# When in an attention step the spread 3x3 operations are handed to the vector engine

## The chip, the cores and the metric

The kernel runs on one core of a Trainium2 chip. The metric is the device time of one execution in microseconds; the time before is the median of three runs, 3276.86 us (3268.33 to 3284.32). The core has a matrix engine (PE in the profile, with its weight loads as PEld), a vector engine (DVE), a scalar engine (ACT), a GpSimd engine (POOL) and a sync engine (SP) that only issues DMAs here.

## The reference, cut to what matters

Eight images of 512 channels and 32x32 pixels, all in float32. Layer 0 adds to the image a block that works on its group norm; layer 1 adds a masked 1x1 convolution of the group norm of that sum. The change touches only the inner part of layer 0, which runs twice per image (two blocks):

```
for i in range(N):                       # N = 2 blocks
    yi = ys[-1]
    z = cbs(yi, m_cv1_w[i], m_cv1_bn[i], 1)              # 3x3 convolution, norm, SiLU
    z = bot_attention(z, m_qkv_w[i], m_rw[i], m_rh[i])   # 4 heads, 1024 tokens
    z = silu(bn_eval(conv2d(z, m_cv2_w[i], 0), m_cv2_bn[i]))
    ys.append(yi + z)
```

The attention takes softmax over 1024 keys of `q (k + r) / 8` and multiplies with `v`. The 3x3 convolution has 256 channels in and out.

## The kernel before, in words

**Slots and units.** The work is cut into 16 slots, one for each image and block, in the order (image p, block 0), (image p+1, block 0), (image p, block 1), (image p+1, block 1) for each of the four pairs of images. Each slot has four attention units: a pair of heads `hp` and one half of the queries. While the units of one slot run, the convolutions of the next slot and of other images fill the matrix engine in between.

**A unit.** `top` transposes the running maxima (`mx`) on the matrix engine into a PSUM tile `mt`, and the vector engine reduces it to `nm` (L513, L514). `spread` brings these maxima back over the partitions as `mb` (L521). Then there are four steps, t = 0, 2, 4, 6, of two key tiles each. A step emits, in this order: `soften` of two tiles of this unit (the vector engine adds `mb`, L525; the scalar engine takes the exponential, L526; GpSimd adds to the sum `acc`, L531), `values` of the step before (matrix engine into `po`, L537), and `logits` of two tiles of the next unit: four matmuls `lg` (L494), each into its own PSUM bank, four scalar copies `st<-lg` (L500), and four maxima on the vector engine, `mx = max(mx, lg)` (L505; none for the first tile). A bank is free again once its copy and its maximum have read it. There are five such banks (`ps_f`), shared with all convolutions.

**The fill.** After each step `advance` runs a generator of other work until a share of the slot is done. That work is conv3 (the 3x3 convolution), the projections to q, k and v, `conv_m2`, and background items of other images (L175 for all 1x1 convolutions, L297 for the 3x3 products).

**The 3x3 convolution.** It is done in a Winograd form along the rows. `transform` computes eight vector operations, `a`, `b`, plane 1 and plane 2 (L264 to L267), then `a2`, `b2`, plane 3 and plane 4 (L269 to L272). `conv3` multiplies six planes in turn with `product`. After product 4, four more vector operations combine results (L340 to L343); L351 and L355 add products 0 and 5.

**Clock and Spread.** The order in which the program is written out is steered by a planner's clock. `clock.tick(us)` moves it on and calls everything that has fallen due. The operations of `transform` and of the combination are a `Spread`: each is put on the clock with its own due time (`delay + gap * n`), so that they don't come in one burst, and `upto` calls those that are needed before they are due. Group norm parts (`mean`, `var`, `norm_x` with L165) are put on the clock too. Most scheduling of instructions within an engine is then done by the tile framework from the order of emission, but the vector operations of `soften`, `logits` and `Spread` are chained in the order in which they were emitted:

```
def in_turn(instruction):
    if turn:
        tc.add_manual_dep(instruction.ins, turn.pop().ins.name, IN_ORDER, reason="order of VectorE")
    turn.append(instruction)
```

Other names that matter below: L441 and L139 add a residual and take its statistics in `conv2`; L471 adds a residual in `last` and reads its PSUM bank; L556 and L558 divide by the sum.

## Time and profile before

| | before |
|---|---|
| median of three runs | 3276.86 us |
| the profiled execution | 3278.47 us |
| its span on the core | 3276.7 us |
| PE busy | 3159.1 us (96%), 11716 matmuls |
| DVE busy | 2045.9 us (62%), 2717 instructions |
| ACT busy | 1756.6 us (54%), 2369 instructions |
| POOL busy | 1219.1 us (37%), 971 instructions |
| granted clock of the matrix engine | 0.99 |

Idle time of PE is what remains of the span, 117.6 us. A line of the waits view names an engine and its line, what ended the wait, and then the total in us, the number of times and the longest. A line of the timeline has start, length in us, engine, source line, operation, tiles, a count of merged instructions, and in brackets the idle time before the first and what ended it. The length of matmuls is modelled.

The slots are periodic: after the first pair of images, the same pattern comes again every 734 us or so (for instance the same transposes `mt` start after the same wait at 1205.1, 1940.7 and 2673.0 us).

### The profile page before, as it was taken

How to read it: one execution, taken by the hardware profiler on the slowest of the kernel's cores; microseconds unless marked ns; L12 is line 12 of the kernel's file. 1: busy time of each engine (PE TensorE's matmuls, PEld its weight loads, DVE VectorE, ACT ScalarE, POOL GpSimd, SP SyncE). 2: the span in 40 equal slices, each digit the busy share in tenths (PEclk: the TensorE clock that was granted, in tenths of full speed). 3: DMA queues.
4: the chain of work that ended last, by engine and by line, in shares of the span. 5: the costliest groups of instructions: out<-in, count | busy, mean ns of one | idle time of the engine just before them, and what ended most of it. 6: DMA issues, size and time to landing. Idle time of an engine off the chain costs nothing.

```text
span 3276.7 us, 33257 instructions
## 1 busy us (share of the span) xinstructions
PE 3159.1 (96%) x11716; PEld 1538.0 (47%) x11716; DVE 2045.9 (62%) x2717; ACT 1756.6 (54%) x2369; POOL 1219.1 (37%) x971
## 2 busy tenths in 40 slices
PE   7999999998999999999999999999999999999998
PEld 3645345353545445354545445354445444453343
DVE  5436566666666575767666675767656676666642
ACT  3245765854545655644545555644655554646631
POOL 2104433335334343344334343444334433444420
PEclk9999999999999999999999999999999999999999
DMA  8752352330323241423323341423333341423366
GB/s 292 275 171 71 119 170 94 116 106 20 121 98 106 75 148 55 161 84 106 122 98 105 104 144 54 161 84 108 124 105 108 101 141 49 160 71 116 111 217 205
DMA packets 142007, 399.30 MB, mean 122 GB/s; under 512 B 13072, under 2 KB 14352, under 8 KB 141840
## 3 DMA queue, kind: packets, MB, share of 16 engines
q1 hardware_dynamic: 141120, 396.94, 36.1%
q8 instruction: 93, 1.52, 0.2%
q14 instruction: 74, 0.61, 0.1%
q10 hardware_dynamic: 720, 0.23, 0.0%
HBM read 317.42 MB, written 79.69 MB: 121 GB/s over the span
## 4 chain that ended last, share of the span: by engine, by line
PE 69%; DVE 11%; issue 5%; ACT 4%; DMA 4%; POOL 1%; POOLq 0%; SPq 0%; ACTq 0%; DVEq 0%
PE cv L175 14%; PE m L297 12%; PE po L537 11%; PE lg L494 10%; PE qk L175 6%; PE l L175 5%; PE v L389 3%; DVE st L525 3%; PE mt L513 2%; PE m L175 2%; DVE rb L556 2%; DVE mx L505 2%; PE den L549 2%; PE mb L521 2%; DMA x<-in_x 1%
## 5 line engine op out<-in xcount | busy, mean ns | idle before, releaser
L531 POOL TENSOR_TENSOR sum<-sum,st 128x512 f32<-128x512 f32 x768 | 973.9, 1299 | 771.5 <-ACT st L526 771.5
L526 ACT ACTIVATE st<-st 128x1024 f32<-128x1024 f32 x512 | 534.3, 1056 | 471.4 <-DVE st L525 464.8
L505 DVE TENSOR_TENSOR mx<-mx,lg 128x512 f32<-128x512 f32 x768 | 479.3, 681 | 434.1 <-ACT st L500 433.6
L500 ACT COPY st<-lg 128x512 f32<-128x512 f32 x1024 | 528.1, 594 | 246.1 <-PE lg L494 189.9
L525 DVE TENSOR_TENSOR st<-st,mb 128x1024 f32<-128x1024 f32 x512 | 604.2, 1213 | 79.8 <-PE mb L521 79.8
L297 PE MATMUL m<-plane,w_m 128*128 128x256 f32 x2304 | 534.0, 386 | 18.0 <-DVE z L351 8.3
L494 PE MATMUL lg<-q,k 64*128 64x512 f32 x2048 | 534.6, 618 | 10.4 <-ACT rb L551 3.3
L537 PE MATMUL po<-st,v 128*64 128x512 f32 x2048 | 509.5, 609 | 17.2 <-ACT st L526 11.4
L297 PEld LDWEIGHTS m<-plane,w_m 128*128 128x128 f32 x2304 | 431.4, 191 | 142.7 <-issue 40.8
L531 POOL TENSOR_TENSOR sum<-st,st 128x512 f32<-128x512 f32 x128 | 162.2, 1288 | 834.1 <-ACT st L526 712.0
L175 PE MATMUL cv<-y,w_cv 128*128 128x512 f32 x1024 | 466.5, 600 | 4.9 <-DVE mx L505 2.1
L494 PEld LDWEIGHTS lg<-q,k 64*128 64x128 f32 x2048 | 188.9, 186 | 346.2 <-issue 236.5
L175 PEld LDWEIGHTS cv<-y,w_cv 128*128 128x128 f32 x1024 | 185.5, 190 | 252.0 <-issue 231.6
L537 PEld LDWEIGHTS po<-st,v 128*64 128x64 f32 x2048 | 125.2, 136 | 327.6 <-issue 231.6
L556 DVE RECIPROCAL rb<-rb 128x256 f32<-128x256 f32 x128 | 216.1, 1725 | 66.0 <-ACT rb L551 66.0
L175 PE MATMUL cv<-x,w_cv 128*128 128x512 f32 x512 | 242.2, 622 | 12.3 <-DVE mx L505 4.1
L175 PE MATMUL l<-x,w_l 128*128 128x512 f32 x512 | 235.2, 604 | 9.6 <-DVE mx L505 6.2
L175 PE MATMUL qk<-z,w_qkv 128*128 128x512 f32 x512 | 234.2, 600 | 1.6 <-DVE mx L505 1.6
L514 DVE TENSOR_REDUCE nm<-mt 128x4 f32<-128x512 f32 x128 | 83.0, 685 | 221.5 <-PE mt L513 221.2
L130 ACT ACT_TABLE_LOAD x122 | 156.5, 1283 | 14.7 <-PE m L175 6.4
L175 PEld LDWEIGHTS cv<-x,w_cv 128*128 128x128 f32 x512 | 97.0, 197 | 138.7 <-issue 112.1
L175 PEld LDWEIGHTS l<-x,w_l 128*128 128x128 f32 x512 | 93.3, 191 | 133.6 <-issue 106.5
(144 smaller groups left out, 2342.1 us busy)
## 6 DMA issues: line engine op xcount, KB each, us to landing
w_m<-w_m SPq DMA_DIRECT2D x96, 768.0 KB, 4.4
w_cv<-in_cv SPq DMA_DIRECT2D x90, 512.0 KB, 3.5
y<-y SPq DMA_DIRECT2D x64, 512.0 KB, 4.7
x<-in_x SPq DMA_DIRECT2D x56, 512.0 KB, 5.2
y<-y SPq DMA_DIRECT2D x64, 256.0 KB, 3.6
k<-r SPq DMA_DIRECT2D x32, 512.0 KB, 3.8
res<-y SPq DMA_DIRECT2D x32, 512.0 KB, 4.2
xr<-in_x SPq DMA_DIRECT2D x32, 512.0 KB, 4.3
```

The lines of the kernel that those rows point to most:

```text
L130: nc.scalar.activation(dst, src, AF.Silu, bias=bn_b[:, col : col + 1], scale=bn_s[:, col : col + 1])
L175: nc.tensor.matmul(ps, w, moving, start=(n == 0), stop=(n == len(terms) - 1))
L297: nc.tensor.matmul(ps[:, ts(co, 256)].rearrange("p (t x) -> p t x", x=F), w[:, co, c, dx], u[:, 9 * c : 9 * c + 8, dx : dx + F], start=(j ...
L389: nc.tensor.matmul(ps[:, ts(j, P)], z[:, c, ts(4 * j4 + j, P)], w[:, c, 512 + P * hp : 512 + P * hp + P], start=(c == 0), stop=(c == IT - 1),)
L494: nc.tensor.matmul(lg[h], self.k[r, ts(t, P)], self.q[r, self.hp, ts(self.half, HALF)], start=True, stop=True)
L500: nc.scalar.copy(st[:, h], lg[h])
L505: in_turn(nc.vector.tensor_tensor(self.mx[:, h], so_far[:, h], lg[h], ALU.max))
L525: in_turn(nc.vector.tensor_tensor(st, st, flat(self.mb), ALU.add))
L526: nc.scalar.activation(st, st, AF.Exp)
L531: nc.gpsimd.tensor_tensor(self.acc[:, h], so_far[:, h], self.st[t][:, h], ALU.add)
L537: nc.tensor.matmul(self.po[HD * h : HD * h + HD], self.v[:, t, ts(h, HD)], self.st[t][:, h], start=(t == 0), stop=(t == KT - 1),)
L556: nc.vector.reciprocal(self.rb[:, r], self.rb[:, r])
```

## The change

In the loop over the steps, the clock was moved on by 2.0 us after `values` and by another 2.0 us after `logits`. Now it is moved on once, after both. An operation that falls due during the first 2.0 us used to be emitted between `values` and `logits`; it is now emitted after `logits`, so behind its four maxima in the chain of the vector engine. The planner's time at the end of the step is the same.

```
                 if t:
                     u.values(t - 2)
                     u.values(t - 1)
-                    clock.tick(2.0)
                 if nxt:
                     nxt.logits(t)
                     nxt.logits(t + 1)
-                    clock.tick(2.0)
+                clock.tick((2.0 if t else 0.0) + (2.0 if nxt else 0.0))
                 advance((base + 4 + t) / steps)
```

More of the change, by code (lines that the diff above doesn't have):

```diff
@@ L1024, in conv_preact_kernel @@
                     u.values(t - 1)
-                    clock.tick(2.0)
                 if nxt:
@@ L1028, in conv_preact_kernel @@
                     nxt.logits(t + 1)
-                    clock.tick(2.0)
+                clock.tick((2.0 if t else 0.0) + (2.0 if nxt else 0.0))
                 advance((base + 4 + t) / steps)
```

## The prediction

> **What bounds the kernel now.** I read the page first, then the waits of PE, then the timeline at every place where the change moves an instruction.

> ```profile
> span 3276.7 us, 33257 instructions
> PE 3159.1 (96%) x11716; PEld 1538.0 (47%) x11716; DVE 2045.9 (62%) x2717; ACT 1756.6 (54%) x2369; POOL 1219.1 (37%) x971
> ...
> L505 DVE TENSOR_TENSOR mx<-mx,lg 128x512 f32<-128x512 f32 x768 | 479.3, 681 | 434.1 <-ACT st L500 433.6
> ```

> PE is the bound: it is idle for 117.6 us of the span, and only that can be won. The maxima mostly wait for the copy of the same bank (433.6 of 434.1 us), so an operation in front of them often costs nothing. The waits of PE:

> ```profile
> PE mt L513 <- DVE mx L505: 10.7, 3, 3.6
> PE m L297 <- DVE z L351: 8.3, 8, 2.1
> PE l L175 <- DVE mx L505: 6.2, 5, 1.5
> PE cv L175 <- DVE mx L505: 6.2, 6, 2.5
> PE m L297 <- DVE mx L505: 6.2, 5, 1.8
> ```

> With three smaller rows (1.6, 1.0 and 0.7) PE waits 32.6 us for maxima, because they free a bank or feed the transposes. That is the pool for the gain; a later operation of the vector engine can add to it.

> [...] L269 takes 712 ns at least and 1802 ns at most, the latter beside the sums L531 (about 1.1 us of waiting, then its own 0.7).

> **The change, part by part.** It adds and removes no instruction. In the built instruction lists, 30 of 2717 vector instructions move behind four maxima (4 x 0.6 us), in 18 places; POOL's and SP's queues, with all DMAs, are unchanged, ACT has swaps in seven places, PE a few. The other Spread operations fall due in the fill. I group the places by pattern and work each from the timeline, letting each operation start when the queue ahead, its copies (L500) and the lock allow. PE's gate (the matmul whose wait stands in brackets) after minus before is the price.

> *Three places at 1200, 1935, 2668 (L269 and L270 moved).*

> ```profile
> 2666.99 0.68 DVE L441 TENSOR_TENSOR xr<-xr,cv2s 128x512 f32<-128x512 f32 x1
> 2667.60 1.80 DVE L269 TENSOR_TENSOR a<-ybuf 128x544 f32<-128x544 f32 x1
> 2669.32 0.68 DVE L139 BATCH_NORM_STATS2 st_b<-xr 128x6 f32<-128x512 f32 x1
> 2669.92 1.18 DVE L270 TENSOR_TENSOR b<-ybuf 128x544 f32<-128x544 f32 x1
> 2671.03 2.47 DVE L505 TENSOR_TENSOR mx<-mx,lg 128x512 f32<-128x512 f32 x4
> ...
> 2672.95 1.97 PE L513 MATMUL mt<-ident,mx 128*128 128x128 f32 x8 [3.56 <-DVE mx L505]
> ```

> PE waits 3.56 us for the third maximum. Without L269 and L270 (1.80 + 1.18, less overlap) L139 ends at 2668.3, the copies (from 2668.07) are ready at 2668.6, and the maxima start at 2668.7 instead of 2671.0: 2.3 us. Behind them L269, L270, L271, L272 end at about 2675.0, so the reductions L514 end 0.2 us later than before, but the matmul that needs them (`mb`) stands behind 12 products (4.6 us) and doesn't wait. Gain 3 x 2.3 = 6.9.

> *Three places at 1375, 2110, 2842 (L265, L266).*

> ```profile
> 2848.10 2.48 DVE L505 TENSOR_TENSOR mx<-mx,lg 128x512 f32<-128x512 f32 x4 [3.42 <-ACT st L500]
> ...
> 2854.87 2.34 DVE L525 TENSOR_TENSOR st<-st,mb 128x1024 f32<-128x1024 f32 x2
> 2857.13 2.47 DVE L505 TENSOR_TENSOR mx<-mx,lg 128x512 f32<-128x512 f32 x4
> ...
> 2857.87 1.35 PE L297 MATMUL m<-plane,w_m 128*128 128x256 f32 x5 [1.35 <-DVE mx L505]
> ```

> Here the moved pair ran in a hole: the maxima waited 3.42 us for copies anyway, so they gain nothing. Behind them the pair takes 2 x 0.7, and from 2850.5 to 2859.6 the queue is full. The next maxima come 1.4 us later, and the PE gate at 2857.87 with them. Loss 3 x 1.4 = 4.1.

> *Two places at 1508, 2242 (L266, L267).*

> ```profile
> 2244.54 5.92 POOL L531 TENSOR_TENSOR sum<-sum,st 128x512 f32<-128x512 f32 x4 [3.18 <-ACT st L526]
> ...
> 2246.08 1.54 DVE L269 TENSOR_TENSOR a<-ybuf 128x544 f32<-128x544 f32 x1
> 2247.55 1.79 DVE L270 TENSOR_TENSOR b<-ybuf 128x544 f32<-128x544 f32 x1
> ...
> 2254.59 1.98 PE L175 MATMUL l<-x,w_l 128*128 128x512 f32 x4 [1.46 <-DVE mx L505]
> ```

> Before, L266 and L267 ran free (0.64 us apart) ahead of the sums. Afterwards the maxima are 1.3 us earlier, but PE waits for no bank there except one l matmul that the list moves ahead (its 0.85 us is lost again at the next gate). L266, L267, L269 and L270 then alternate with the four sums, at 1.6 to 1.75 each; L272 ends 1.95 us later, and so do L525, the next maxima and the gate. Loss 2 x 1.95 = 3.9.

> *Three places at 944, 1681, 2415 (L267).* The queue's tail keeps its end within 0.1 us (the lock only changes its victim). The first copy of the next step is moved ahead of an exponential, so the first maximum doesn't wait 0.46 us for it, and the gate (0.70) comes 0.45 earlier. Gain 1.4.

> *Four places at 505, 1428, 2162, 2896 (L341, and L351 one L525 earlier).* L341 to L343 end 0.8 us later behind the lock, L351 stands one L525 (1.13) earlier: PE's gate on L351 (0.65) comes 0.3 earlier. The second exponential and its copies are 1.4 later, but 24 products (5.4 us) cover that. Gain 1.3.

> *At 454 (L265, L266):* the exponentials come 0.9 to 1.2 later, but a copy is moved in front of the table load, and the gate (1.78) opens 0.7 earlier. *At 657 (L269, L270):* the maxima waited 1.97 us for copies; the reductions end 1.3 later, just covered by 12 products: 0. *At 772 to 806 (L264, L267, L271):* L525 comes 0.8 and then 2.1 later, partly behind POOL's release of buffers, and PE's gates on the exponential (4.44 and 3.04) about 1.1 in sum. *At 246* three L165 go behind copies on ACT; PE doesn't wait: 0.

> Sum: 6.9 + 1.4 + 1.3 + 0.7 - 4.1 - 3.9 - 1.1 = 1.2 us saved. The profiled execution would be 3278.5 - 1.2 = 3277.3; it is 1.6 above the median of the runs shown, so **3275.7** for the median. That is no change: 0.5% (16.4 us) is about what a measurement of this kernel can tell from none, and the three runs alone span 15.9.

> Bounds of what I can't see: the first group gives 0 (if the `nm` reductions become the gate) to 10.7 (the whole wait); the losses 0 (hidden after all) to about twice (a second gate); the stretch at 772, where ACT, POOL and DVE wait in turn, 2 us gained to 5 lost.

> **The rivals.** *Tails hidden.* If the second, third and last terms of loss cost nothing, 1.2 + 9.1 = 10.3 is saved: 3266.6. For it speaks that DVE is busy for only 62%; against it that at these places its queue has no hole until the gate. Over 0.5% needs 16.4 of 32.6 us, more than the gated time that moves; only scatter takes it there.

> *Tails gate (slower).* The postponed operation lands beside the four sums of its step, is locked out for 1.1 us, and the next L525, exponential, copy, maximum and bank come 1.95 later as at 2242. This passes 0.5% when 9 of the 18 places pay 1.95 and the gains are eaten; with 10, 3276.9 + 19.5 = 3296.4. For it speak PE's waits behind full queues; against it that I find locked tails with a gate in two places, unlocked ones in three.

> *Nothing moves that counts.* Order changes, gates don't: 3276.9. Only 1% of the vector instructions move. It can't be told from my forecast and shares its chance.

> **How the numbers follow.** Forecast with the null case 0.56; tails hidden 0.22, of which 0.06 lies beyond 0.5%; tails gate 0.22, of which 0.16 does. So faster 0.06, same 0.78, slower 0.16. The range runs from 3264 (tails hidden and a little scatter) to 3291 (tails gate at 7 places): 8 in 10.

> **What would show it.** Right: the waits of PE for `mx` at `mt` (3 x 3.57) fall to about 1.2 each; the waits at 1390, 2124, 2858 grow from 1.35 to about 2.8, those at 1521, 2255 from 1.47 to about 3.4 (less any lead that PE has by then, or more by it). Busy times of PE, ACT and POOL stay. Wrong: if the places at 505 or 944 lose time, if PE's idle time in sum changes by over 10 us, or if a wait appears away from the 18 places.

## The result and the profile after

The changed kernel takes **3287.2 us** (median of 8 runs, 3283.8 to 3294.3) against 3279.6 us before (8 runs, 3268.3 to 3284.3). The ratio is 1.0029 [1.0016, 1.0042]: slower by 9.5 us [5, 14], where the forecast was 1.2 us faster. (Microseconds beside a ratio are the ratio times the median before; the two medians alone differ by 7.6.) The change is smaller than the 0.5% that the prediction took for the least that can be told from none, but with eight runs on each side it is a loss and not a null.

From the page of the kernel after, its span, the busy times and the group of the maxima:

```profile
span 3283.5 us, 33262 instructions
...
PE 3167.8 (96%) x11716; PEld 1535.8 (47%) x11716; DVE 2044.9 (62%) x2717; ACT 1757.7 (54%) x2369; POOL 1216.6 (37%) x971
...
L505 DVE TENSOR_TENSOR mx<-mx,lg 128x512 f32<-128x512 f32 x768 | 480.2, 682 | 449.5 <-ACT st L500 449.2
```

The idle time of PE, span less busy time, fell from 117.6 to 115.7 us, in sum nearly as forecast. But its **busy** time rose by 8.7 us with the same 11716 matmuls. So the loss isn't in waiting: the same matmuls take longer. The waits of PE after (what ended the wait, total us, times, longest):

```profile
PE m L297 <- DVE mx L505: 9.7, 5, 2.7
...
PE lg L494 <- DVE x2r L471: 6.2, 2, 3.1
...
PE mt L513 <- DVE mx L505: 3.7, 3, 1.2
PE mb L521 <- DVE nm L514: 3.5, 3, 1.2
```

The wait of `mt` has gone from 10.7 to 3.7 us, that of L297 for maxima has grown from 6.2 to 9.7. Two rows are new: `lg` waits for L471 (6.2 us), and `mb` for the reductions (3.5 us).

**Where busy time grows.** A stop is idle time of PE in front of a matmul. The timeline at the third place of 1375/2110/2842 shows the stop, first before:

```profile
2857.87 4.15 PE L297 MATMUL m<-plane,w_m 128*128 128x256 f32 x18 [1.35 <-DVE mx L505]
```

Then in the kernel after, with the windows view for the clock behind the stop (columns: stretch, us, busy us and count of PE, PEld, DVE, ACT, POOL; then granted clock, DMA share, GB/s):

```profile
2857.22 1.98 PE L175 MATMUL l<-x,w_l 128*128 128x512 f32 x4
2861.95 5.84 PE L297 MATMUL m<-plane,w_m 128*128 128x256 f32 x18 [2.75 <-DVE mx L505]
```

```profile
2862.90:2866.30 3.40, 3.40 (x9) 2.70 (x8) 1.50 (x4) 0.00 (x0) 3.40 (x3) 0.50 0.04 14
2866.40:2870.40 4.00, 4.00 (x23) 2.44 (x22) 0.65 (x5) 0.00 (x0) 0.00 (x0) 1.00 0.00 0
```

Before, the same 18 products took 4.15 us after a stop of 1.35 us. After a stop of 2.75 us they take 5.84: the granted clock is 0.50 for 3.4 us, which I call a window of half clock, and half of that is lost (5.84 - 4.15 = 1.7). So 1.4 us of stop cost 3.1 us of time.

To price every place, I took the same matmul ahead of it and behind it in both traces. The stretch between them divides into idle time, the loss to the half clock (half of PE's busy time in windows with a granted clock of 0.50), and the rest (busy time less that loss). These are differences of the two profiled executions in us; negative is time saved:

| places | forecast | measured | idle | half clock | rest |
|---|---|---|---|---|---|
| 1200, 1935, 2668 | -6.9 | -9.1 | -3.5 | -7.3 | +1.7 |
| 1375, 2110, 2842 | +4.1 | +9.1 | +4.4 | +4.8 | -0.1 |
| 1508, 2242 | +3.9 | +7.4 | +1.5 | +6.8 | -1.0 |
| 772 to 806 | +1.1 | +3.1 | -1.6 | +0.5 | +4.1 |
| 944, 1681, 2415 | -1.4 | -1.6 | -1.6 | 0 | 0 |
| 505, 1428, 2162, 2896 | -1.3 | -1.6 | -1.6 | 0 | 0 |
| 454 | -0.7 | -0.4 | -0.7 | 0 | +0.3 |
| 657 | 0 | +0.2 | 0 | 0 | +0.2 |
| sum of these places | -1.2 | +7.0 | -3.1 | +4.8 | +5.2 |
| first to last matmul compared | | +7.0 | -1.7 | +2.0 | +6.7 |

What lies away from these places comes to nothing in sum, but out of parts: +1.4 of idle time, -2.8 of half clock and +1.5 of rest. Windows of half clock come and go there too: in all there are 14 before and 16 after, of 67.8 and 67.7 us. So the half clock is not longer in total. The change moves it: the losses at 1375, 1508 and 772 with their like (12.1 us) are largely offset by the gain at 1200 and its like (7.3) and by windows elsewhere. Most of the net growth of busy time is the rest, of which 4.1 us stand at 772. Where the +1.7 at 1200 and its like and the +1.5 elsewhere come from, I did not follow.

### The profile page after: what moved, and what is told of

Read it like the earlier page. It is cut to its first block, busy times and chain, and to the rows that moved or that the text cites. A ratio compares the mean times of both kernels' runs of the same rounds, so it can differ in the third digit from the quotient of the medians.

```text
span 3283.5 us, 33262 instructions
## 1 busy us (share of the span) xinstructions
PE 3167.8 (96%) x11716; PEld 1535.8 (47%) x11716; DVE 2044.9 (62%) x2717; ACT 1757.7 (54%) x2369; POOL 1216.6 (37%) x971
## 4 chain that ended last, share of the span: by engine, by line
PE 70%; DVE 10%; issue 5%; ACT 5%; DMA 3%; POOL 0%; POOLq 0%; ACTq 0%; SPq 0%; DVEq 0%
PE cv L175 14%; PE m L297 12%; PE po L537 12%; PE lg L494 11%; PE qk L175 6%; PE l L175 5%; PE v L389 3%; DVE st L525 2%; PE mt L513 2%; PE m L175 2%; PE den L549 2%; PE mb L521 2%; DVE mx L505 2%; DVE rb L556 2%; ACT st L526 1%
## 5 line engine op out<-in xcount | busy, mean ns | idle before, releaser
L531 POOL TENSOR_TENSOR sum<-sum,st 128x512 f32<-128x512 f32 x768 | 970.6, 1295 | 780.4 <-ACT st L526 780.4
L526 ACT ACTIVATE st<-st 128x1024 f32<-128x1024 f32 x512 | 534.4, 1056 | 469.7 <-DVE st L525 462.9
L505 DVE TENSOR_TENSOR mx<-mx,lg 128x512 f32<-128x512 f32 x768 | 480.2, 682 | 449.5 <-ACT st L500 449.2
L500 ACT COPY st<-lg 128x512 f32<-128x512 f32 x1024 | 528.4, 594 | 271.5 <-PE lg L494 222.5
L525 DVE TENSOR_TENSOR st<-st,mb 128x1024 f32<-128x1024 f32 x512 | 605.2, 1215 | 67.6 <-PE mb L521 67.6
L494 PE MATMUL lg<-q,k 64*128 64x512 f32 x2048 | 543.1, 620 | 16.3 <-DVE x2r L471 6.2
L297 PE MATMUL m<-plane,w_m 128*128 128x256 f32 x2304 | 536.9, 387 | 20.9 <-DVE mx L505 9.7
L297 PEld LDWEIGHTS m<-plane,w_m 128*128 128x128 f32 x2304 | 432.7, 192 | 146.9 <-issue 43.8
L531 POOL TENSOR_TENSOR sum<-st,st 128x512 f32<-128x512 f32 x128 | 162.2, 1288 | 843.3 <-ACT st L526 710.7
L175 PE MATMUL cv<-y,w_cv 128*128 128x512 f32 x1024 | 466.6, 600 | 3.6 <-DMA y<-y 1.7
L175 PEld LDWEIGHTS cv<-y,w_cv 128*128 128x128 f32 x1024 | 185.3, 190 | 251.1 <-issue 230.1
L175 PE MATMUL cv<-x,w_cv 128*128 128x512 f32 x512 | 236.5, 609 | 12.2 <-DVE mx L505 4.1
L175 PE MATMUL l<-x,w_l 128*128 128x512 f32 x512 | 240.6, 617 | 6.6 <-DVE mx L505 3.5
L175 PE MATMUL qk<-z,w_qkv 128*128 128x512 f32 x512 | 234.2, 600 | 1.7 <-DVE mx L505 1.7
L514 DVE TENSOR_REDUCE nm<-mt 128x4 f32<-128x512 f32 x128 | 83.0, 685 | 221.7 <-PE mt L513 221.7
L175 PEld LDWEIGHTS l<-x,w_l 128*128 128x128 f32 x512 | 96.0, 196 | 134.8 <-issue 112.9
L175 PEld LDWEIGHTS cv<-x,w_cv 128*128 128x128 f32 x512 | 94.9, 194 | 136.9 <-issue 109.0
```

What stands on the lines that cost most here:

```text
L175: nc.tensor.matmul(ps, w, moving, start=(n == 0), stop=(n == len(terms) - 1))
L297: nc.tensor.matmul(ps[:, ts(co, 256)].rearrange("p (t x) -> p t x", x=F), w[:, co, c, dx], u[:, 9 * c : 9 * c + 8, dx : dx + F], start=(j ...
L494: nc.tensor.matmul(lg[h], self.k[r, ts(t, P)], self.q[r, self.hp, ts(self.half, HALF)], start=True, stop=True)
L500: nc.scalar.copy(st[:, h], lg[h])
L505: in_turn(nc.vector.tensor_tensor(self.mx[:, h], so_far[:, h], lg[h], ALU.max))
L525: in_turn(nc.vector.tensor_tensor(st, st, flat(self.mb), ALU.add))
```

## The experiments

Theory: (1) a stop of PE of about 2 us or more (2.75 us above; 2.12 us at 1046 in the same trace) is followed by a window of half clock, so a stop has a second price that the waits don't show; (2) at 772 to 806 the order of PE breaks pairs of half-width matmuls. Rival: the losses are what the stops' lengths say, and the rest is scatter. All of the first four experiments have one edit, in the loop over steps; only the set differs (slot, unit, step):

```
+                late = (s, j, t) in LATE
                 if t:
...
-                    clock.tick(2.0)
+                    if not late:
+                        clock.tick(2.0)
...
+                if late:
+                    clock.tick((2.0 if t else 0.0) + (2.0 if nxt else 0.0))
```

**Only the gaining places** (454, 505 and its like, 944 and its like, 1200 and its like).

```
+    LATE = {(1, 0, 4), (1, 1, 4), (6, 1, 4), (10, 1, 4), (14, 1, 4), (3, 3, 2),
+            (7, 3, 2), (11, 3, 2), (5, 0, 6), (9, 0, 6), (13, 0, 6)}
```

> Only the places at 454, the four with L341, the three with L267 alone and the three with L269 and L270 in front of the transposes are emitted late; all others as before. Theory (the price of each place adds up, and a stop of PE that is long enough is followed by matmuls at half clock): PE gains 9.1 + 1.7 + 1.6 + 0.4 = 12.8 us in the profile, some 3266 us against 3279. Rival (the places don't add up, the change costs through something global such as the clock at random): within 4 us of before.

Measured: 3263.5 us, ratio 0.9966 [0.9953, 0.9978], or 11.1 us faster [7, 15]. By place: -9.2 (idle -3.5, half clock -7.3, rest +1.7) at 1200 and its like, then -1.7, -1.6 and -0.4. The stretch at 772, which this kernel leaves alone, is 1.3 us shorter. In its trace the first stop there (1.94 us, as before) is followed by half clock, so that the next eight `po` take 3.40 instead of 2.02 us; but the stop behind them shrinks from 4.44 to 3.06. This window cost nothing, as PE would have waited anyway.

**Only the hole** (1375, 2110, 2842).

```
+    LATE = {(6, 0, 4), (10, 0, 4), (14, 0, 4)}
```

> Only the three places at 1375, 2110 and 2842 (L265 and L266, which ran in a hole) are late. Theory (longer stop and then half clock): the stop of PE before L297 is 2.75 us instead of 1.35 at each, followed by a half-clock window of 3.4 us, and the cost is 3 x 3.0 = 9 us. Rival (the wait alone costs): 3 x 1.4 = 4.2 us.

Measured: 3289.3 us, ratio 1.0044 [1.0031, 1.0056]. The three places cost 9.1 us: 4.1 of idle time and 5.1 of half clock, with one window of 3.41 us after each stop of 2.74 or 2.75 us. The ratio says 14.4 us [10, 18]; what lies beyond the 9.1 is not at these places (the profiled execution, the slowest of the five, has more windows elsewhere, too), and I can't say whether it comes from the change.

**Only the locked tails** (1508, 2242).

```
+    LATE = {(6, 3, 2), (10, 3, 2)}
```

> Only the two places at 1508 and 2242 (L266 and L267, which end up beside the sums of GpSimd) are late. Theory: the stop moves to the logits behind L471, is 3.1 us long and is followed by half clock: 2 x 3.7 = 7.4 us. Rival (the wait alone): idle time of PE grows by 2 x 0.8 and the cost is 1.6 us; the prediction had 3.9.

Measured: 3284.0 us, ratio 1.0021 [1.0012, 1.0029], or 6.9 us. The two places cost 7.1: 1.5 of idle time, 6.6 of half clock, -1.0 of rest. So the theory held, and the wait alone (1.6) is far too little. The timeline of the kernel after (the whole change) shows the second of the places, PE first and then DVE:

```profile
2250.22 1.98 PE L494 MATMUL lg<-q,k 64*128 64x512 f32 x6
2255.27 2.07 PE L494 MATMUL lg<-q,k 64*128 64x512 f32 x2 [3.07 <-DVE x2r L471]
2257.27 7.81 PE L175 MATMUL l<-x,w_l 128*128 128x512 f32 x12
...
2251.13 1.78 DVE L269 TENSOR_TENSOR a<-ybuf 128x544 f32<-128x544 f32 x1
2252.83 1.78 DVE L270 TENSOR_TENSOR b<-ybuf 128x544 f32<-128x544 f32 x1
2254.54 0.68 DVE L471 TENSOR_TENSOR x2r<-l,x2r 128x512 f32<-128x512 f32 x1
```

L471 empties the PSUM bank that the last two `lg` need. It stands behind four operations that take turns with GpSimd's sums (L266, L267, L269, L270: 1.59 to 1.79 us each, where L269 takes 0.71 at least in the trace of before; the four L531 from 2247.64 take 6.39 us, where one takes 1.295 in the mean). The ends alternate, 0.6 us from that of a sum to that of the next operation and 1.1 from there to that of the next sum; this is what the prediction calls the lock. So L471 comes at 2254.5. Before, it came behind two of them. The two short stops of 0.85 and 1.46 us have become one of 3.07, and that one is followed by 6.8 us of half clock (granted clock 0.50 from 2255.30 to 2262.12).

**Only the crowded stretch** (772 to 806).

```
+    LATE = {(2, 3, 2), (2, 3, 4), (2, 3, 6)}
```

> Only the three steps at 772, 783 and 791 are late. Theory (the order of PE that comes with it breaks pairs of half-width matmuls of logits and values): PE idles no more than before and PE's busy time grows; cost 3 us. Rival (a later chain of exponentials): the stops in front of the values grow from 4.4 and 3.0 us; cost 1.1 us or more, as idle time.

Measured: 3282.0 us, ratio 1.0013 [1.0003, 1.0022], or 4.3 us. The stretch costs 3.0 us: idle -1.6, half clock +0.5, rest +4.1. PE in the kernel after, where before had `po` x8 and then `lg` x6 behind the stop of 4.44 us (the first line is from ahead of it, at full clock; from 777.33 to 784.16 the clock is 0.50):

```profile
768.70 1.12 PE L494 MATMUL lg<-q,k 64*128 64x512 f32 x2
...
776.83 1.52 PE L537 MATMUL po<-st,v 128*64 128x512 f32 x4 [4.09 <-ACT st L526]
778.29 2.07 PE L494 MATMUL lg<-q,k 64*128 64x512 f32 x2
780.29 1.98 PE L537 MATMUL po<-st,v 128*64 128x512 f32 x4
782.20 2.08 PE L494 MATMUL lg<-q,k 64*128 64x512 f32 x4
```

`lg` use 64 rows and `po` 64 columns (64*128 and 128*64 in these lines, where those of L297 have 128*128); I call them matmuls of half width. Each matmul has two records in the trace (2048 `lg` for 1024 in the program), so two `lg` are one head and four are both heads of a key tile, on different rows: a pair. At full clock eight `lg` in a row take 1.99 us and four mostly 1.13, but two alone take 1.12 as well, and four `po` alone 1.08 where eight take 1.94. In these traces one head's `lg` without its partner thus cost as much as both together.

**The crowded stretch with the order of PE held.** As above, and the `lg` and `po` of three steps are chained in the order in which they are emitted.

```
+    CHAIN = {(2, 3, 4), (2, 3, 6), (3, 0, 2)}
+                chain["on"], chain["last"] = (s, j, t) in CHAIN, None
...
+            if chain["last"] is not None:
+                tc.add_manual_dep(instruction.ins, chain["last"].ins.name, IN_ORDER, reason="pairs on TensorE")
+            chain["last"] = instruction
```

> As the kernel with only the steps at 772, 783 and 791 late, but PE's logits and values of the steps at 783, 791 and of the one after the next unit's start are chained in the order in which they are emitted, so that no pair of half-width matmuls is broken. Theory (broken pairs): the price of the stretch falls from 3.0 to about 1 us. Rival (late exponentials): it stays at 3 or grows.

Measured: one run, 3279.7 us, so the place is read from its trace:

```profile
772.17 3.44 PE L545 MATMUL po<-st,v 128*64 128x512 f32 x8 [3.00 <-ACT st L534]
775.54 1.99 PE L502 MATMUL lg<-q,k 64*128 64x512 f32 x8
781.31 3.11 PE L545 MATMUL po<-st,v 128*64 128x512 f32 x8 [3.79 <-ACT st L534]
```

The eights are back, and the rest falls from +4.1 to +0.15 us: that part of the loss was the broken pairs. (The first and the third line ran partly at half clock.) But the stretch still costs 2.0 us, not about 1. The first stop is now 3.00 us instead of 1.94, because no `lg` slips in ahead of it, and a window of half clock follows it. Of the 2.0, 0.5 is idle time and 1.4 half clock. So the run confirms the broken pairs and misses on the sum.

**The hole, filled.** As "only the hole", but with two more matmuls with zero weights at each of the three places (four records in the trace), into the bank that the projection `l` has open; they add nothing to it.

```
+        for n, (w, moving) in enumerate(fill):
+            nc.tensor.matmul(ps, w, moving, start=False, stop=(n == len(fill) - 1))
...
+                    fill = [(zeros, xn[1][:, 1])] * 2 if (n, h, cp, c) in FILL else ()
```

> As the kernel with only the places at 1375, 2110 and 2842 late, but at each of them two more matmuls by a block of zeros are added to the l bank that is open just before the stop of 2.75 us. Theory (a long stop of PE brings a window at half clock): the stop shrinks to about 0.8 us, no window at half clock follows at these three places, and although PE does 12 more instructions the price of the three places falls from 9.1 to 4.2 us. Rival (the half clock has other causes): the windows stay and the price with them.

Measured: 3281.5 us, ratio 1.0009 [1.0002, 1.0015], or 2.9 us [0.7, 4.9] instead of 14.4. The timeline at the third place, and the clock behind it:

```profile
2854.16 1.88 PE L179 MATMUL l<-x,ybuf 128*128 128x512 f32 x4
2857.06 4.15 PE L299 MATMUL m<-plane,w_m 128*128 128x256 f32 x18 [1.03 <-DVE mx L508]
```

```profile
2857.00:2861.00 4.00, 3.94 (x18) 3.48 (x19) 2.52 (x6) 0.50 (x1) 4.00 (x4) 1.00 0.29 107
```

The products are as late as in "only the hole" (the maxima haven't moved), but they take 4.15 us again, at full clock. The three places cost 3.7 us instead of 9.1: 5.1 of added work, -1.4 of idle time and no half clock. Against the kernel with the open hole, useless work on the engine that is the bound saves time, and that is the strongest evidence that the second half of the price is the clock and not the wait.

**Half of the hole** (only L266 late at these places, L265 early).

```
-                    clock.tick(2.0)
+                    clock.tick(1.0 if late else 2.0)
...
+                if late:
+                    clock.tick(3.0)
```

> At the same three places only L266 is late, L265 stays ahead. Theory: the stop is 2.05 us. If that is too short for the half clock, the price is 3 x 0.7 = 2.1 us; if it is always long enough, 7.0. Stops of 1.35 us never brought a window so far, stops of 2.75 always, those of 2.12 in some executions: I expect something in between, and not the same at all three. Rival (the price goes with the stop alone): 2.1 us, no windows.

Measured: 3283.8 us, ratio 1.0017 [1.0008, 1.0026], or 5.6 us. The stops are 1.98 us. The first is followed by no window, the other two are, as the second here:

```profile
1390.77 4.15 PE L297 MATMUL m<-plane,w_m 128*128 128x256 f32 x18 [1.98 <-DVE mx L505]
2125.48 5.84 PE L297 MATMUL m<-plane,w_m 128*128 128x256 f32 x18 [1.98 <-DVE mx L505]
```

The prices are -0.2, 2.5 and 2.3 us. So at about 2 us the half clock comes in some cases and not in others, and the price jumps instead of growing with the stop. The last section says what tells these cases apart.

**The gains, with the reductions let ahead.** As "only the gaining places", but at 1200, 1935 and 2668 the planner's due items are held until the next unit begins, so that L272 comes behind the reductions L514.

```
-            while self.due and min(d for d, _ in self.due) <= self.now:
+            while not self.held and self.due and min(d for d, _ in self.due) <= self.now:
...
+                if (s, j, t) in HOLD:
+                    clock.held = True
...
+            clock.held = False
```

> As the kernel with only the gaining places late; in addition the clock is held at the three places with L269 and L270 until the transposes and reductions of the next unit are emitted, so that L272 comes behind L514. Theory: the stop of PE for L514 before mb falls from 1.2 to about 0.5 us at each, 2 us less than without, some 0.4% under before. Rival (something else gates mb): no change against the gaining places alone.

Measured: 3258.8 us, ratio 0.9944 [0.9930, 0.9958], or 18 us faster [14, 23]. It is faster than before and after. Against the gains alone the two intervals touch (0.9958 and 0.9953), so what the hold itself gives is read from the trace:

```profile
2657.58 1.25 PE L521 MATMUL mb<-ident,nm 128*128 128x128 f32 x8 [0.53 <-DVE nm L514]
```

`mb` waits 0.53 us where it waits 1.15 to 1.17 us in the kernel with the gains alone, and the three places give 11.1 us instead of 9.2. The stretch at 772 is 1.3 us shorter here too, again with half clock behind its first stop.

The four parts, run alone, cost -12.9, +9.1, +7.1 and +3.0 us by their places, +6.3 together; the whole change costs +7.0. So by place the parts add up, nearly. By the ratios they add to +14.5 us, with 5.3 of the surplus in the hole alone, against 9.5 [5, 14] for the whole change; what happens away from the places isn't accounted for.

## Why the prediction was wrong

**What held, and what was luck.** The sum was a sum of idle time, and as such it came near: 1.2 us less forecast, 1.7 less measured between the first and the last of the matmuls compared. Much of that is luck. The idle time at 1200 and its like fell by 3.5 and not 6.9, at 1508 and 2242 it grew by 1.5 and not 3.9, at 772 it fell by 1.6 where 1.1 more was forecast, and away from the places it grew by 1.4; the misses cancel. The single waits were better founded. The wait of `mt` fell to 1.23 us three times (1.2 forecast), the waits at 1390, 2124 and 2858 grew to 2.75 (2.8 forecast). The places at 944, 505 and 454 gave 1.6, 1.6 and 0.4 us (1.4, 1.3 and 0.7 forecast).

**The step that failed: a stop was priced at its length.** "PE's gate (the matmul whose wait stands in brackets) after minus before is the price" leaves out what the matmuls behind the gate take. The half clock behind stops stands in no term of the sum. Three terms were mis-sized by it:

- *1375, 2110, 2842.* The extra stop was 1.4 us, as said, but the term of 4.1 measured 9.1. The filled hole (3.7 us at these places, no half clock) against the open one (9.1, of which 5.1 half clock) shows that the difference is the clock.
- *1508, 2242.* The forecast had the stop at an `l` matmul behind the maxima and longer by 1.95 us. In the trace it is at `lg`, whose bank is freed by L471; I had not followed that operation's place behind the lock. The idle time grew by less than forecast (1.5 instead of 3.9), and half clock made it 7.4.
- *1200, 1935, 2668.* Here the same error lay on the other side. The stops of 3.57 us before each brought 3.4 or 6.8 us of half clock, and with the stops these went: -7.3 us that the sum didn't have. That 9.1 us were gained where 6.9 were forecast is this error less the next one.

**`mb` was said not to wait, and it waits 1.17 us three times.** The cover was counted as 12 products of 4.6 us in sum. That is their time at half clock (4.63 us at 2674.71 in the trace of before, where the clock is 0.50 from 2671.7 to 2678.5); at full clock the 12 take 2.76, as here, in the kernel after:

```profile
2676.86 1.25 PE L513 MATMUL mt<-ident,mx 128*128 128x128 f32 x8 [1.23 <-DVE mx L505]
2677.95 2.76 PE L297 MATMUL m<-plane,w_m 128*128 128x256 f32 x12
2681.89 1.25 PE L521 MATMUL mb<-ident,nm 128*128 128x128 f32 x8 [1.18 <-DVE nm L514]
```

The change that takes the stop away also takes away part of the cover. Of 2.3 us a place, 1.17 came back as this wait; the clock more than made up for it. The lower bound in the text ("if the `nm` reductions become the gate") named the mechanism, but I took the other value. Letting L514 ahead of L272 returned 0.6 us a place.

**Swaps on PE were priced at nothing.** At 772 to 806 the idle time fell by 1.6 us, where 1.1 of loss was forecast. But "a few" swaps on PE split pairs, and 4.1 us of extra matmul time came of it: the term of 1.1 measured 3.1. With the order held, 3.9 of the 4.1 went.

**Of what would show it right,** "Busy times of PE, ACT and POOL stay" failed for PE (+8.7 us), and the waits at 1521 and 2255 grew at `lg` and not at `l` (3.07). Of what would show it wrong, nothing came true at a size that counts: the new waits of `mb` and `lg` stand at places of the change, and the idle time changed by 2 us. These signs looked at waits and at two groups of gaining places, and so none could tell of a loss in busy time. **Of the rivals,** "tails gate" named the lock at 2242 rightly; its price of 1.95 us a place became 3.7 there, and a locked tail that holds PE up was found at those two places only.

## What to carry to other kernels

Where PE is the bound, price a stop as its length plus what the clock takes after it: in this case nothing at 1.35 us, about 1.7 us in some cases at 2 us, and 1.7 to 3.4 us at the stops of 2.75 and 3.07 us looked at, less what falls into a later stop. Two stops of 0.85 and 1.46 us cost no half clock where one of 3.07 did, so it can pay to split a stop, or to put a few matmuls with zero weights into a long one. Don't take the cover of a wait from matmuls that ran at half clock in the old trace, and look at every swap on PE that parts matmuls of half width (4.1 us at 772 here).

## What the hardware showed that I had not expected

Of the stops looked at one by one, none of 1.35 us was followed by a window of half clock; of those of 1.98 us two of three were; of 2.74 or 2.75 us all six, and of 3.07 or 3.08 us all four. The windows lasted 3.41 us (7 in the trace of before, 11 in that of after) or 6.83 (6 and 4), but for one in each that the end of the trace cuts off; why some last twice as long, I did not find. A window begins now a little before the end of a stop (at 1384.90 in the kernel after, where the stop ends at 1385.04) and now about 1 us behind it (at 2862.87, where it ends at 2861.95).

```profile
1051.04 5.45 PE L297 MATMUL m<-plane,w_m 128*128 128x256 f32 x24 [2.12 <-DVE z L351]
```

```profile
1046.27 7.14 PE L297 MATMUL m<-plane,w_m 128*128 128x256 f32 x24 [2.12 <-DVE z L351]
```

Before, an edge of the grid at 1050.35 cuts the stop into 1.43 and 0.69 us, no window follows, and the 24 products take 5.45 us. After, the stop lies whole between the edges at 1043.57 and 1046.98, a window starts at 1046.98, and they take 7.14. In the half of the hole the first stop of 1.98 us is cut into 0.28 and 1.70 us and has no window; the other two are whole and have one. Over the ten traces, from the first record of the clock to the last matmul, all 88 steps at full clock with at least 2.0 us of idle time (1.99 rounded) are followed by half clock, 10 of them in the trace of before and 11 in that of after. Of 83 steps with 1.0 to 1.91 us of it, and at most 0.05 us of `lg`, `po`, `den`, `mt` and `mb`, none is (8 and 5 of them in these two traces). By my estimate from the 2.0 and the 3.41 us, whether a stop between 2 and nearly 4 us brings half clock depends on how the grid cuts it, and if every cut is equally likely, a stop of 2.75 us brings it in about two cases of three; then six of six was luck as well. And the half clock at a place in one trace is that of one cut, and not the mean.

Open is what makes less than 2 us enough in some steps. Of 143 steps with 1.0 to 1.95 us idle that also hold some of those matmuls, most of which are of half width, 30 are followed by half clock (in the kernel after, those with the stops of 1.00 us at 1861, 1.73 at 3012 and 1.53 at 582), but one with the same 1.00 us at 2599 is not. And a window of 6.83 us, from 101.44 in the trace of before and from 101.49 in that of after, has no stop ahead of it at all: PE is busy without a gap in the 3.41 us ahead, at matmuls of 16 columns (`rank`, 128x16).
